# A convolution kernel: two of three images combined in place of every second, no image added by VectorE in the middle, and one more weight step after a combined low part

## The chip, the cores and the metric

The kernel runs on one core of one Trainium2 chip. The core has five engines that work side by side and meet through semaphores: TensorE (PE in the profile; PEld is its weight load), VectorE (DVE), ScalarE (ACT), GpSimd (POOL) and SyncE (SP), which only issues transfers here. Each engine runs its own instructions strictly in the order of the program. The metric is the device time of one execution in microseconds (us); lower is better. The time before is 984.07 us, the median of three runs (983.44 to 984.48).

## The reference

The input x has 160 images of 128 channels and 32 x 32 points in fp32. The output is x plus a convolution of the group-normalised x:

```
def _gn(v, G=32, eps=1e-5):
    ...
    return ((g - m) / jnp.sqrt(s + eps)).reshape(v.shape)
...
x = x + _L0_conv_ref(_gn(x), L0_conv_U)
```

The convolution is 3 x 3 with padding 1, from 128 to 128 channels, and there are five sets of weights: each run of 32 images in the kernel's order has its own. The weights are first quantised from U: `s1 = (max - min) / 3`, `v1 = s1 * floor(U / s1)`, `s2 = s1 / 5`, `v2 = s2 * floor((U - v1) / s2)`, `w = v1 + v2`.

## The kernel before, in words

**The work on one image.** The 128 channels lie on the 128 partitions, an image is 1024 elements wide, and two images are one chunk of a pool of 11 chunks. The values that TensorE multiplies are fp16, in two parts: a high part (the rounded value) and a low part (what the rounding left), each of which is multiplied with the weights. An image is handled in one of two ways, which `combined` (L607) chooses.

- A *direct* image: GpSimd normalises it into z (L670) or ScalarE does (L596, for the first images of a group), ScalarE rounds it to hi (L604), VectorE subtracts to lo (L699) and makes four quarters of sums and differences of its rows (L712, L720, L721). The high part is convolved directly: 18 matmuls at L736. The low part goes through the four quarters: 12 matmuls at L791.
- A *combined* image: the sums and differences are made before the split. GpSimd makes the edge columns (L634) and one difference (L664), VectorE the rest (L646 and L653), into a tile v of 2048 elements. ScalarE scales and rounds it to vh (L686), VectorE makes the low part vl (L692). Both parts go through the quarters: 24 matmuls at L791, and none at L736.

Of the quarters, two fill the PSUM banks m1 and m2 first (`sums_of_pairs`, L802). ScalarE copies half of m2 out (L839), and VectorE writes the sum and the difference of the two into the image's pair of banks eo (`pairs`, L848 and L850), into which `main` (L826) adds the rest. There are two such pairs of banks.

**The residual.** When an image's banks are done, one of two things happens (`by_hand`, L861, and `residual`, L868). Most images: ScalarE copies eo into a tile sum (L876), and GpSimd issues an accumulating transfer that adds sum to the image in its chunk (L899). By hand: VectorE adds eo to the image (L893). By hand are the first three, the last four, and, from image 31, every eighth. When both images of a chunk are done, SyncE stores it (L904) and loads a new one into a chunk that is free (L455).

**Statistics and weights beside the images.** ScalarE measures images ahead of their use (L202 for the mean, L209 for the square; a few by VectorE, L192). For groups of 8 images small steps on TensorE, VectorE (L257 to L270) and GpSimd (L247) make the scale. The weights of the next set are quantised on VectorE, one step at a time: `make_column` (L495) yields 14 steps for each of three columns (L101 to L127 and L507), `sums_of_set` (L544) six more (L531 to L533). The generator of these steps is called `later`, and `take(later, 1)` puts one step into VectorE's order. `later` begins at the third image of a set (the fifth in the first set), and what is left four images before the set's end is put there at once.

**The order.** One loop over the 160 images (L1039) writes all engines' instructions. The iteration of image i holds TensorE's matmuls of image i, and for VectorE in this order: the low part of image i + 2, with weight steps between, any addition by hand of image i - 1, the pair operations of image i + 1, and the sums of image i + 4 if that one is combined (or one more weight step if not). GpSimd's work for image i + 4 (`beside_pairs`, L657) is chained by `after` (L675) to the last low-part or weight step of VectorE ahead of the pair operations, so that it runs beside these; so is rstd (`power`, L245), which GpSimd does ahead of it. ScalarE's order is: measure a coming image, copy the sum of image i - 1, copy m2 of image i + 1, round the high part of image i + 3, square the coming image. SyncE's order is: store the chunk that ended at image i - 2, then load.

Of the kernel before, what the change touches and what calls it, by code (L numbers as in the profile page):

```python
# [22 lines left out]
LAST = 4  # L23
# [112 lines left out]
def last_of(steps, last=None):  # L136
    for last in steps:
        pass
    return last


def run(steps):

    while True:
        try:
            next(steps)
        except StopIteration as end:
            return end.value
# [133 lines left out]
def general_path(tc, keep, steps, x, u, out):  # L282
# [8 lines left out]
    with tc.If(far > 0), ExitStack() as ctx:  # L291
# [9 lines left out]
        for n in range(N_SETS):  # L301
            un = one.tile([P, C, TAPS], F32, tag="u", name=f"g_u{n}")
            nc.sync.dma_start(un, uv[n])
            wn = one.tile([P, C, TAPS], F32, tag="w", name=f"g_w{n}")
            k1, k2 = run(steps.quantise(one, un, f"g{n}", F32))
            nc.vector.tensor_scalar_mul(wn, k1, steps.s1)
            nc.vector.scalar_tensor_tensor(wn, k2, steps.s2, wn, ALU.mult, ALU.add)
# [38 lines left out]
class Main:  # L346
# [25 lines left out]
    LOAD_LEAD = 18  # L372
    STEADY = 7
    BY_VECTOR = (8, 10, 11, 14, 19, 24, 29, 34)
    FIFTHS = 126
    THIRDS = 146
    EARLY = 8
    FIRST = 3
    HURRIED = (0, 2, 4, 8, 24)
# [173 lines left out]
    def keep_sums(self, n, col):  # L553
        wt = self.wts[n, col]
        run(self.both_sums(
            self.nc.gpsimd, wt[:, self.SUM], wt[:, self.DIFF], *(wt[:, k] for k in range(ROW))
        ))
        if col == self.COLS[-1]:
            run(self.sums_across(n, self.nc.gpsimd))
# [47 lines left out]
    def combined(self, i):  # L607

        if i < self.STEADY or i >= self.imgs:
            return False  # L610

        if i < self.FIFTHS:
            return i % 2 == 1
        return (i - self.FIFTHS) % 5 % 2 == 0 if i < self.THIRDS else i % 3 != 1

    def by_scalar_too(self, i):

# [243 lines left out]
    def by_hand(self, i):  # L861


        if i < self.FIRST or i >= self.imgs - LAST:
            return True
        return i > self.BY_VECTOR[-1] - 4 and i % 8 == 7

    def residual(self, i):  # L868

# [38 lines left out]
    def run(self):  # L908
# [49 lines left out]
        def take(steps, count, last=None):  # L958
            for _ in range(count):
                last = next(steps, None) or last  # L960
            return last

        def measure(stage, *images):
            for i in images:
                self.measure(i, (stage,))
# [72 lines left out]
        later, turned = iter(()), []  # L1038
        for i in range(self.imgs):  # L1039
# [35 lines left out]
            if n + 1 < N_SETS:  # L1075
                if b == (2 if n == 0 else 0):
                    self.load_set(n + 1)
                if b == (4 if n == 0 else 2):
                    later = (s for col in self.COLS for s in self.make_column(n + 1, col))
# [3 lines left out]
            if i < self.FIRST:  # L1083

                if i == 0:
                    measure(0, 8, 9, 10)
                    self.normalise(4)
                    self.high_part(4)
                if i == 2:
                    self.leave(3)  # L1090
                    self.normalise(5)
                    measure(1, 9)
                    self.high_part(5)
                    self.pairs(3)
                    measure(0, 11)
                    self.low_part(4)
                    run(self.combinations(4))
                self.residual(j)
            else:

                last = None
                if self.combined(i + 2):
                    last = last_of(self.low_combined(i + 2))
                elif i + 2 < self.imgs:
                    self.low_part(i + 2)
                    take(later, 1)
                    last = last_of(self.combinations(i + 2))
                last = take(later, 1, last)
                for st in scaled:
                    self.after(st.power(), last)  # L1110
                if i + 4 < self.imgs:
                    self.beside_pairs(i + 4, last)
                if i > self.FIRST and self.by_hand(j):
                    self.residual(j)
                for k in by_scalar:
                    self.measure(k, (0,))
                if i > self.FIRST and not self.by_hand(j):
                    self.residual(j)
                    self.accumulate(j)
                part = i + 3 < self.imgs and not self.combined(i + 3)  # L1120
                if i + 1 < self.imgs:
                    self.leave(i + 1)
                for st in ready:
                    if not st.late:
                        st.deviations()
                if part:
                    if self.by_scalar_too(i + 3):
                        self.normalise(i + 3)
                    self.high_part(i + 3)
                if self.combined(i + 3):  # L1130
                    self.high_combined(i + 3)
                for k in by_scalar:
                    self.measure(k, (1,))
# [8 lines left out]
            for n_of, col in turned:  # L1142
                self.keep_taps(n_of, col)
                if col == self.COLS[-1]:
                    later = self.sums_of_set(n_of)
# [78 lines left out]
```

## Time and profile before

| what | us |
|---|---|
| median of three runs | 984.07 |
| the profiled execution's own time | 984.48 |
| its span, first to last instruction | 982.8 |
| images 35 to 138, an image on average (from the starts of L848) | 5.8 |
| start: first start of L848 (image 3) | 60.1 |

The page gives the busy time of each engine over the span, the chain of work that ended last, followed back from the last instruction, and groups of instructions: line, engine, operation, what is written and read, shapes, count, total busy time, mean of one, and the idle time of the engine just ahead of them with what ended it. The trace also gives busy times by stretch, and the waits: who waited, for what, microseconds in total, times, and the longest. A busy share is a mean over the stretch; two engines that both show nearly the whole stretch run beside each other.

### The profile page before, as it was taken

What the parts mean: (1) busy time and instruction counts of PE and PEld (TensorE: products, weight loads), DVE (VectorE), ACT (ScalarE), POOL (GpSimd) and SP (SyncE); (2) the same over time, 40 slices, a digit from 0 to 9 for tenths busy, and PEclk for the clock granted to TensorE, in tenths of its full rate; (3) what the DMA queues carried; (4) which work ended last, traced back from release to release, by engine and by line L of the source; (5) the groups of instructions that cost most, each with busy time, mean ns of one, the idle gap of its engine ahead of it and who ended that gap; (6) DMA issues with size and microseconds to landing.
All of it is one profiled execution on the core that took longest, in us unless ns stands there. A gap on an engine that the chain in (4) does not pass through costs nothing.

```text
span 982.8 us, 13226 instructions
## 1 busy us (share of the span) xinstructions
PE 944.5 (96%) x4504; PEld 442.2 (45%) x4504; DVE 913.2 (93%) x1332; ACT 830.4 (84%) x1135; POOL 355.7 (36%) x441
## 2 busy tenths in 40 slices
PE   2989999999999999999999999999999999999997
PEld 1434444444444444444444444444444444444443
DVE  7979999997999999889999998999999998989995
ACT  5759998889998998998998989898898989898551
POOL 4344423533343333333333433333333434343430
PEclk9999999999999999999999999999999999999999
DMA  9527899999998989998989999998989998997775
GB/s 354 218 84 190 219 257 256 252 267 268 279 281 268 250 262 267 265 318 229 290 222 281 240 275 270 287 258 257 258 262 246 269 265 241 316 236 202 179 205 163
DMA packets 65117, 245.86 MB, mean 250 GB/s; under 512 B 5008, under 2 KB 5008, under 8 KB 65040
## 3 DMA queue, kind: packets, MB, share of 16 engines
q1 hardware_dynamic: 45312, 173.09, 50.4%
q0 software_dynamic: 19728, 71.84, 38.1%
q8 instruction: 37, 0.61, 0.2%
q14 instruction: 40, 0.33, 0.1%
HBM read 89.19 MB, written 83.89 MB: 176 GB/s over the span
## 4 chain that ended last, share of the span: by engine, by line
PE 75%; DVE 11%; issue 4%; DMA 4%; ACT 3%; POOL 2%; SPq 0%; DVEq 0%; POOLq 0%; ACTq 0%
PE eo L736 25%; PE eo L791 24%; PE m L791 12%; PE m1b L791 8%; PE m1a L791 5%; DMA xt<-in_x_dram 2%; DVE v L646 2%; DVE vl L692 2%; DVE lo L699 1%; DVE eo L848 1%; DMA xt<-sum 1%; DMA range<-in_L_conv_U_dram 1%; POOL rstd L247 1%; DVE v L653 1%; ACT vh L686 1%
## 5 line engine op out<-in xcount | busy, mean ns | idle before, releaser
L736 PE MATMUL eo<-hi,wt 128*128 128x496 f16 (+2 forms) x1386 | 370.5, 378 | 0.9 <-ACT wt L527 0.9
L791 PEld LDWEIGHTS <-wt 128*128 128x128 f16 x1884 | 184.2, 99 | 209.9 <-DVE eo L850 1.1
L736 PEld LDWEIGHTS <-wt 128*128 128x128 f16 x1458 | 143.3, 100 | 165.9 <-issue 3.8
L202 ACT ACTIVATE junk<-xt 128x1024 f16<-128x1024 f32 x152 | 160.6, 1057 | 42.2 <-DMA xt<-in_x_dram 39.1
L692 DVE SCALAR_TENSOR_TENSOR vl<-v,rstd,vh 128x2048 f16<-128x2048 f32 x82 | 192.3, 2345 | 1.7 <-ACT vh L686 1.5
L876 ACT COPY sum<-eo 128x1024 f32<-128x1024 f32 x137 | 142.7, 1042 | 50.6 <-PE eo L791 50.4
L791 PE MATMUL eo<-vh,wt 128*128 128x496 f16 (+1 forms) x492 | 184.5, 375 | 0.3 <-DVE eo L850 0.3
L791 PE MATMUL eo<-vl,wt 128*128 128x496 f16 (+1 forms) x492 | 184.4, 375 | 0.0
L209 ACT ACTIVATE junk<-xt,mv 128x1024 f16<-128x1024 f32 x152 | 174.6, 1149 | 0.1
L791 PE MATMUL eo<-rows,wt 128*128 128x496 f16 (+1 forms) x450 | 171.6, 381 | 0.0
L686 ACT ACTIVATE vh<-v,rstd 128x2048 f16<-128x2048 f32 x82 | 164.1, 2001 | 7.3 <-DVE v L653 6.6
L791 PEld LDWEIGHTS <-across 128*128 128x128 f16 x984 | 96.2, 98 | 118.7 <-issue 7.9
L670 POOL TENSOR_SCALAR z<-xt,ngm,rstd 128x1024 f32<-128x1024 f32 x53 | 62.5, 1180 | 227.0 <-DVE rows L721 39.6
L634 POOL TENSOR_SCALAR v<-xt,ngm 128x64 f32<-128x64 f32 x82 | 30.7, 374 | 257.5 <-issue 73.6
L899 POOL DMA_DIRECT2D xt<-sum x137 | 119.6, 876 | 6.5 <-ACT sum L876 3.9
L839 ACT ACTIVATE m<-m 128x512 f32<-128x512 f32 x157 | 93.9, 598 | 22.9 <-PE m L791 16.6
L646 DVE TENSOR_TENSOR v<-xt 128x960 f32<-128x960 f32 x82 | 105.0, 1281 | 2.3 <-POOL v L634 2.3
L791 PE MATMUL m<-vl,across 128*128 128x496 f16 (+1 forms) x246 | 92.2, 375 | 4.4 <-DVE vl L692 4.3
L699 DVE TENSOR_TENSOR lo<-z,hi 128x1024 f16<-128x1024 f32 x78 | 95.0, 1217 | 0.0
L791 PE MATMUL m<-vh,across 128*128 128x496 f16 (+1 forms) x246 | 92.2, 375 | 1.1 <-ACT m L839 1.1
L664 POOL TENSOR_TENSOR v<-xt 128x512 f32<-128x512 f32 x82 | 84.7, 1032 | 0.0
L604 ACT CAST hi<-z 128x1024 f16<-128x1024 f32 x78 | 81.5, 1045 | 0.8
(144 smaller groups left out, 1156.9 us busy)
## 6 DMA issues: line engine op xcount, KB each, us to landing
xt<-in_x_dram SPq DMA_DIRECT2D x78, 1024.0 KB, 9.8
out_dram<-xt SPq DMA_DIRECT2D x78, 1024.0 KB, 5.9
xt<-sum POOLq DMA_DIRECT2D x137, 512.0 KB, 6.3
u<-in_L_conv_U_dram SPq DMA_DIRECT2D x4, 576.0 KB, 9.1
xt<-in_x_dram SPq DMA_DIRECT2D x4, 512.0 KB, 9.8
range<-in_L_conv_U_dram SPq DMA_DIRECT2D x3, 576.0 KB, 8.1
out_dram<-xt SPq DMA_DIRECT2D x3, 512.0 KB, 2.7
u<-in_L_conv_U_dram SPq DMA_DIRECT2D x2, 288.0 KB, 3.1
```

Of the source, the lines that this page charges most:

```text
L202: self.nc.scalar.activation(junk, image, ACTF.Copy, scale=-1.0 / image.shape[1], accum_out=self.mv[:, j, 0:1],)
L209: self.nc.scalar.activation(junk, image, ACTF.Square, bias=self.mv[:, j, 0:1], accum_out=self.mv[:, j, 1:2],)
L646: nc.vector.tensor_tensor(self.view(v, 1, (511, 2), (half, H), (1, half - 1)), self.view(x, 1, (1, 2), (W, H), (2, half - 1)), self.view(x ...
L664: ins = nc.gpsimd.tensor_sub(self.v[i][:, 1536:], odd, even)
L686: self.nc.scalar.mul(vh, self.v[i], st.rstd[:, j])
L692: yield self.nc.vector.scalar_tensor_tensor(vl, self.v[i], st.rstd[:, j], self.hi[i], ALU.mult, ALU.subtract)
L699: self.nc.vector.tensor_sub(lo[:, 1 : self.H + 1, :].rearrange("p h w -> p (h w)"), self.z.pop(i), self.hi[i].rearrange("p h w -> p (h w)"),)
L736: nc.tensor.matmul(self.bank(target, a)[:, first:end, c0:c1], self.wts[n, col][:, k, :], tile[:, s0 : s0 + 2 * (end - first) - 1 : 2, c0 + ...
L791: self.nc.tensor.matmul(out, weights, moving, start=start and j == 0, stop=False, skip_group_check=True)
L839: self.nc.scalar.mul(m2, self.m2_ps, 0.5)
L876: nc.scalar.copy(self.as_banks(i, self.sum[i]), self.flat(i, eo))
L899: self.nc.gpsimd.dma_start(self.image(i), self.sum.pop(i), accum_op=ALU.add)
```

## The change

The choice of combined images becomes one rule for all images from the eighth on: i % 3 is not 1. Before it was every odd image to 125, then three of five to 145, then the same rule as now. `by_hand` loses its middle: images 31, 39, 47 and so on to 151 go through ScalarE's copy and the accumulating transfer like the others. After the low part of a combined image two weight steps are taken in place of one; after a direct one it stays at two (one between the low part and its quarters, one behind them). GpSimd's instructions of `beside_pairs` and `power` stay chained to the last of these.

```diff
     def combined(self, i):
...
-        if i < self.FIFTHS:
-            return i % 2 == 1
-        return (i - self.FIFTHS) % 5 % 2 == 0 if i < self.THIRDS else i % 3 != 1
+        return i % 3 != 1
...
     def by_hand(self, i):
-        if i < self.FIRST or i >= self.imgs - LAST:
-            return True
-        return i > self.BY_VECTOR[-1] - 4 and i % 8 == 7
+        return i < self.FIRST or i >= self.imgs - LAST
...
-                last = take(later, 1, last)
+                last = take(later, 2 if self.combined(i + 2) else 1, last)
                 for st in scaled:
                     self.after(st.power(), last)
                 if i + 4 < self.imgs:
                     self.beside_pairs(i + 4, last)
```

The constants `FIFTHS = 126` and `THIRDS = 146` go, since nothing reads them.

More of the change, by code (lines that the diff above doesn't have):

```diff
@@ L374 @@
     BY_VECTOR = (8, 10, 11, 14, 19, 24, 29, 34)
-    FIFTHS = 126
-    THIRDS = 146
     EARLY = 8
```

## The prediction

> **What bounds the kernel now.** I read the page from the top: the busy shares first, then the chain that ended last, then the busy times by stretch, because the shares are means over stages with different limits.
>
> ```profile
> span 982.8 us, 13226 instructions
> PE 944.5 (96%) x4504; PEld 442.2 (45%) x4504; DVE 913.2 (93%) x1332; ACT 830.4 (84%) x1135; POOL 355.7 (36%) x441
> PE 75%; DVE 11%; issue 4%; DMA 4%; ACT 3%; POOL 2%; SPq 0%; DVEq 0%; POOLq 0%; ACTq 0%
> ```
>
> TensorE holds three quarters of the chain, but VectorE is only 3 points less busy. The stretches below (stretch, then PE, PEld, DVE, ACT and POOL busy with counts, clock, DMA share, GB/s) say where each one decides.
>
> ```profile
> 67.00:163.00 96.00, 92.92 (x449) 43.56 (x448) 94.24 (x155) 85.38 (x118) 36.81 (x44) 1.00 0.86 236
> 163.00:258.00 95.00, 93.35 (x448) 43.69 (x447) 87.02 (x127) 84.79 (x119) 36.86 (x46) 1.00 0.99 268
> 443.00:581.00 138.00, 138.00 (x664) 64.64 (x663) 135.81 (x201) 124.66 (x174) 49.27 (x57) 1.00 0.94 260
> 581.00:628.00 47.00, 47.00 (x227) 22.13 (x226) 40.44 (x57) 43.14 (x59) 16.48 (x19) 1.00 0.98 278
> ```
>
> The last two rows are one set of 32 images (185 us, 5.78 us an image). For about 24 images the next set's weights are quantised on VectorE between the images: TensorE is full, and VectorE is idle for only 2.2 us of 138. For the other 8, VectorE has 6.6 us free in 47. So the middle is bound by TensorE with VectorE 2% behind it, and in 67 to 163 VectorE is already the fuller one. The change takes from the first and gives to the second, so its whole worth hangs on that 2%.
>
> **The change part by part.** The groups that it touches (line, engine, operation, shapes, count; busy us and mean ns; idle before):
>
> ```profile
> L692 DVE SCALAR_TENSOR_TENSOR vl<-v,rstd,vh 128x2048 f16<-128x2048 f32 x82 | 192.3, 2345 | 1.7 <-ACT vh L686 1.5
> L646 DVE TENSOR_TENSOR v<-xt 128x960 f32<-128x960 f32 x82 | 105.0, 1281 | 2.3 <-POOL v L634 2.3
> L699 DVE TENSOR_TENSOR lo<-z,hi 128x1024 f16<-128x1024 f32 x78 | 95.0, 1217 | 0.0
> L653 DVE SCALAR_TENSOR_TENSOR v<-xt,twice 128x512 f32<-128x512 f32 x82 | 60.8, 742 | 0.0
> ...
> L712 DVE TENSOR_TENSOR rows<-lo 128x1024 f16<-128x1024 f16 x75 | 51.3, 684 | 0.8
> L721 DVE TENSOR_TENSOR rows<-lo 128x512 f16<-128x512 f16 x75 | 31.2, 416 | 0.0
> L720 DVE TENSOR_TENSOR rows<-lo 128x512 f16<-128x512 f16 x75 | 31.2, 416 | 0.0
> L893 DVE TENSOR_TENSOR xt<-eo,xt 128x1024 f32<-128x1024 f32 x21 | 25.6, 1217 | 4.3 <-PE eo L791 3.3 <-PE eo L736 1.0
> ```
>
> Back-to-back records overlap by about 0.08 us: in the timeline L692 starts at 354.64 and its successor at 356.90. So I price by the distance from one start to the next: L692 2.26, L646 1.23, L653 0.66, together 4.15 us for a combined image; L699 1.13, L712 0.60, L720 and L721 0.33 each, together 2.40 for a direct one.
>
> *More combined images.* By the old rule 60 images to 125, 12 in 126 to 145 and 10 after are combined: 82, as L692 counts. By the new one, every i from 7 with i % 3 not 1: 102. For each of the 20: TensorE runs 24 matmuls instead of 30. In the chain of waits twelve of them take 2.54 us, so a combined image is 5.08; a direct one is six steps of 0.85 (three L736 and one L791) and six L791 of 0.65 per three, 6.40. That is 1.32 us saved. VectorE pays 4.15 less 2.40, 1.75 us more. ScalarE pays L686 (2.00) for L604 (1.05), 0.95 more. GpSimd pays L634 and L664 (0.37 and 1.03) for L670 (1.18), 0.2 more; at 36% busy that hides. Totals: PE -26, DVE +35, ACT +19.
>
> *None added by VectorE in the middle.* Images 31, 39 and so on to 151, sixteen, lose L893. Its record is 1.22, start to start about 1.35 with its wait on PE: DVE -21 us. In its place come sixteen ScalarE copies (1.04 each, L876: ACT +16), sixteen GpSimd issues (L899, 0.88 each: POOL +14, hidden), and 16 transfers of 512 KB. The 137 of before take 38.1% of 16 engines' 983 us, 2.73 us each, so DMA +44 us. In the present middle the engines are 0.94 to 0.98 busy, so this has little cover.
>
> *One more weight step after a combined low part.* A set has 48 steps (three columns of 14, six sums). Two per image are taken now, alternating 1 and 3; afterwards 7 in three images, so they end after 20.6 images, not 24. Their sum, about 22.5 us a set (0.47 each, from the spacing of L101 to L127, L507 and L531 to L533), is moved, not added. But GpSimd's rstd, edge columns and difference are chained to the last of these steps, and start one step (0.47 us) later. L646 waits for the edge columns; the two pair operations between (1.33 us) cover their 0.37, but not rstd and edges together (1.47 and 0.37). Today that wait is 2.3 us in 4 places. I take +1 us in all; without the pair operations' cover it would be 0.5 us for each of 102 images.
>
> *Buffers* move no wait that I can see: the two v buffers now serve neighbours, but each is read for the last time an iteration before it is written again.
>
> *Sum for one set of the middle* (185.0 us now). VectorE's content apart from the steps in the first 24 images is 135.8 less 22.5, over 24: 4.72 us an image. Add 1.75/6 (half to two thirds combined) and take off 1.35/8: 4.84. Over 20.6 images, with the steps, 122.2 us; the idle share that VectorE has where it is already the fuller (1.8 of 96 us, first row) makes it 124.4. The other 11.4 images: TensorE falls by 1.32/6 to 5.56; ScalarE is at 43.1/8 = 5.39 now and gains 0.16 and 0.13, 5.68 as record time, less as spacing. I take 5.62, 64.1 us. Sum 188.5, so +3.5 for each of three sets, **+10.5**. With no idle share and 5.56 it would be +0.6 a set; with 5% idle and 5.75, +9.
>
> *First set (60 to 259 us).* 18 combined in place of 14: VectorE +7, less 1.35 for image 31, about 4 of it where VectorE is the fuller; the steps brought forward cost it there and are given back after. TensorE's -5 counts only in the second half, which waits elsewhere. **+4** (0 to +8).
>
> *From 813 us on.* One more combined, three adds less, no weight steps: TensorE -1.3 and some of VectorE's -4 where it holds the chain. **-2.5** (-5 to +1).
>
> The total is +12. The profiled execution took 984.48 us, its span 982.8 and 1.7 around it, and 0.4 above the median of 984.07. 984.5 + 12 = **996.5**, so I say **997**. A measurement tells 0.2%, 2 us, from no change.
>
> **Two rules against rows.** The matmuls start every 0.21 us with no gap in 443 to 628, so I count TensorE's saving in full where it decides. The Trainium skill (Perfetto Trace Analysis, Identifying the Most-Contended Engine) warns that matmul busy time is no measure of headroom and wants the weight-load share instead. That is 45% here, and read so, TensorE would not be the limit, the 11.4 images would stay at today's 47/8 = 5.88, 0.26 above my 5.62, and three sets would add 9 us, an estimate of 1006. I follow the starts.
>
> L646's record runs from 1149 to 1989 ns, longer where GpSimd's L664 lies beside it; my 1.23 is a spacing with GpSimd beside it. The Trainium skill (SBUF — State Buffer, Who interferes with whom) says that a VectorE instruction with two SBUF inputs contends with GpSimd's reads; by it the new L646 could cost the upper end, 0.7 us more for 20, +14 us. No row makes that usual.
>
> **The rivals.**
> 1. *VectorE runs ahead* (faster). If its surplus is absorbed by running ahead while TensorE has less to do, a set costs its total only: 176.3 + 5.33 x 1.75 - 4 x 1.35 = 180.2, with today's 2.2 idle 182.4, -2.6 a set; with the first set at 0 and the end at -4 that is 973. For it: VectorE at 98% and TensorE at 100% live beside each other now. Against: its order is fixed, pair operations wait for one of two PSUM pairs, and the 6.6 us free are where no weights are due, images away. It decides when more than 4 us a set are carried over.
> 2. *The accumulating transfers bind* (much slower). SyncE's stores wait for them in order, and the loads stand behind the stores:
>
> ```profile
> SPq L904 <- DMA xt<-sum: 760.4, 84, 16.0
> SPq L455 <- DMA out_dram<-xt: 25.8, 14, 2.6
> ```
>
> and ScalarE's first pass over an image waits for the load (who waited for what: us in total, times, longest):
>
> ```profile
> ACT junk L202 <- DMA xt<-in_x_dram: 39.1, 24, 8.1
> ```
>
> Every fourth chunk now has its last image added by VectorE and catches up there. From 163 to about 240 us every image is accumulated already, and the stretch 163 to 258 shows DMA 0.99, 9.3 us of ScalarE's waits for loads (its waits in that window), TensorE 1.65 us idle and VectorE 8. Four transfers more make a set's DMA 0.95 x 185 + 10.9 = 187 us, above the time it has. If ScalarE's late copies hold VectorE's pair operations for 1.65 to 3 us in 95, that is +10 to +18 over some 570 us of the middle, on top of the forecast's 997 in part, since VectorE waits already there: 1010. Against: the shares reach 1.03 with 310 GB/s elsewhere.
> 3. *The terms cancel*: +0.6 a set, +1 in the first, -3 at the end: 984.
>
> **How the numbers follow.** Forecast 0.50, rival 2 0.22, rival 1 0.17, rival 3 0.11. The forecast's own terms give 986 to 1010; the range reaches down into rival 1 and up to rival 2's figure: 979 to 1012. Faster is 0.17 from rival 1 and 0.02 of rival 3, same 0.08 of rival 3, the rest slower, 0.73.
>
> **What would show it.** L692 x102, L893 x5, L876 x153; matmuls 120 fewer. Right: in a set's first 21 images VectorE without gaps at about 6.0 us an image and TensorE with gaps, then 5.6 an image. Wrong towards faster: TensorE still without gaps with weights in the stretch. Wrong towards slower: L202's waits for loads well above 39 us, or L848 waiting for ScalarE above its 31 us of before.

## The result, and the profile after

The changed kernel takes 1043.7 us (median of four), before takes 983.8: the ratio is 1.061, with a 95% interval of 1.059 to 1.064. The loss is 60 us, and the prediction, which had the direction, put it at 12; the time lies above its range. The lines move by four to six in the new file: L692 is now L688, L646 is L642, L653 is L649, L848 and L850 are L844 and L846, L876 is L870, L899 is L893 and L904 is L898.

The top of the page of after, in the order in which that of before was read:

```profile
span 1041.6 us, 13067 instructions
PE 938.9 (90%) x4384; PEld 427.6 (41%) x4384; DVE 940.6 (90%) x1296; ACT 853.0 (82%) x1139; POOL 382.6 (37%) x489
DVE 45%; DMA 18%; issue 15%; PE 10%; POOL 7%; ACT 4%; SPq 0%; POOLq 0%; ACTq 0%; DVEq 0%
```

TensorE has 120 matmuls fewer (4384 for 4504), as it should, but the chain went from TensorE (75% to 10%) to VectorE (45%) and to transfers (18%). No engine is busier than 90%, so the span is made of stretches with different limits. Here are the stretches of the same images as in the prediction (images 4 to 18 and 19 to 34 of the first set, then 67 to 90 and 91 to 98); columns as there: stretch, length, PE, PEld, DVE, ACT and POOL busy, clock, DMA share, GB/s.

```profile
66.00:174.00 108.00, 96.92 (x448) 43.75 (x446) 103.35 (x162) 87.21 (x117) 37.01 (x49) 0.97 0.80 216
174.00:273.00 99.00, 93.42 (x441) 43.30 (x440) 85.81 (x112) 86.02 (x119) 40.46 (x51) 0.98 0.94 247
472.00:622.00 150.00, 136.25 (x637) 61.34 (x635) 143.29 (x196) 128.25 (x174) 56.15 (x67) 0.99 0.95 254
622.00:672.00 50.00, 47.81 (x219) 21.88 (x219) 40.97 (x52) 45.11 (x60) 17.61 (x21) 0.97 0.99 268
```

Images 67 to 90, most of them beside weight steps, took 138 us and now take 150. TensorE, which had no gap there, has 14 us of them, and VectorE is busy for 143. Images 91 to 98, without weight steps, took 47 and now take 50, though TensorE has less to do there, VectorE is idle for 9, and the DMA engines are at 0.99. These are two different losses, and the experiments were made to part them.

Where the 58.8 us of span came from, by the starts of the pair operations: the part to image 34 took 14.7 us more (1.2 less up to image 3, 15.9 more from there), images 35 to 130, three sets' worth, 41.9 more (554.9 to 596.8), and the rest 2.2 more. The prediction had 4, 10.5 and -2.5.

The groups of VectorE that grew, and the waits that answer to those shown of before:

```profile
L688 DVE SCALAR_TENSOR_TENSOR vl<-v,rstd,vh 128x2048 f16<-128x2048 f32 x102 | 239.2, 2345 | 3.0 <-ACT vh L682 2.7
L642 DVE TENSOR_TENSOR v<-xt 128x960 f32<-128x960 f32 x102 | 136.2, 1336 | 7.2 <-POOL v L630 7.2
L649 DVE SCALAR_TENSOR_TENSOR v<-xt,twice 128x512 f32<-128x512 f32 x102 | 75.7, 742 | 4.3 <-POOL twice L279 4.3
```

```profile
ACT junk L202 <- DMA xt<-in_x_dram: 59.1, 34, 7.8
...
DVE eo L844 <- ACT m L835: 36.9, 25, 3.6
PE m L787 <- DVE vl L688: 36.4, 24, 5.4
...
DVE nnn L101 <- DMA u<-in_L_conv_U_dram: 6.6, 3, 4.0
```

TensorE's wait for the low part was in before:

```profile
PE m L791 <- DVE vl L692: 4.3, 4, 1.3
```

The counts are as forecast (102). One duration is not: the difference that was 1281 ns is 1336. TensorE now waits for VectorE's low part 36 us in 24 places (4.3 in 4 before), and ScalarE's waits for loads went from 39 to 59 us. The load of the next set's U stands in the same queue of SyncE: VectorE's first weight step waits for it three times, which it did not in before.

### The profile page after: what moved, and what is told of

Its sections match the earlier page's. It is cut to its first block, busy times and chain, and to the rows that moved or that the text cites. A ratio compares the mean times of both kernels' runs of the same rounds, so it can differ in the third digit from the quotient of the medians.

```text
span 1041.6 us, 13067 instructions
## 1 busy us (share of the span) xinstructions
PE 938.9 (90%) x4384; PEld 427.6 (41%) x4384; DVE 940.6 (90%) x1296; ACT 853.0 (82%) x1139; POOL 382.6 (37%) x489
## 4 chain that ended last, share of the span: by engine, by line
DVE 45%; DMA 18%; issue 15%; PE 10%; POOL 7%; ACT 4%; SPq 0%; POOLq 0%; ACTq 0%; DVEq 0%
DVE vl L688 11%; DVE v L642 7%; DMA xt<-in_x_dram 7%; DMA xt<-sum 7%; DVE eo L844 5%; DMA u<-in_L_conv_U_dram 4%; PE eo L787 4%; DVE v L649 4%; DVE lo L695 3%; DVE eo L846 3%; PE eo L732 2%; POOL rstd L247 2%; PE m L787 2%; DVE tt L110 1%; POOL v L660 1%
## 5 line engine op out<-in xcount | busy, mean ns | idle before, releaser
L787 PEld LDWEIGHTS <-wt 128*128 128x128 f16 x1884 | 181.8, 99 | 231.8 <-DVE eo L846 15.9
L732 PE MATMUL eo<-hi,wt 128*128 128x496 f16 (+3 forms) x1026 | 273.5, 377 | 2.6 <-DVE eo L846 1.6
L688 DVE SCALAR_TENSOR_TENSOR vl<-v,rstd,vh 128x2048 f16<-128x2048 f32 x102 | 239.2, 2345 | 3.0 <-ACT vh L682 2.7
L787 PE MATMUL eo<-vh,wt 128*128 128x496 f16 (+1 forms) x612 | 230.7, 377 | 4.1 <-DVE eo L846 3.8
L787 PE MATMUL eo<-vl,wt 128*128 128x496 f16 (+1 forms) x612 | 230.6, 377 | 0.0
L682 ACT ACTIVATE vh<-v,rstd 128x2048 f16<-128x2048 f32 x102 | 203.9, 1999 | 31.1 <-DVE v L649 20.8
L202 ACT ACTIVATE junk<-xt 128x1024 f16<-128x1024 f32 x152 | 160.6, 1057 | 62.2 <-DMA xt<-in_x_dram 59.1
L870 ACT COPY sum<-eo 128x1024 f32<-128x1024 f32 x153 | 160.8, 1051 | 40.2 <-PE eo L787 39.8
L732 PEld LDWEIGHTS <-wt 128*128 128x128 f16 x1098 | 106.7, 100 | 127.4 <-DVE eo L846 8.5
L787 PE MATMUL m<-vl,across 128*128 128x496 f16 (+1 forms) x306 | 117.6, 384 | 36.5 <-DVE vl L688 36.4
L642 DVE TENSOR_TENSOR v<-xt 128x960 f32<-128x960 f32 x102 | 136.2, 1336 | 7.2 <-POOL v L630 7.2
L893 POOL DMA_DIRECT2D xt<-sum x153 | 133.6, 873 | 10.6 <-ACT sum L870 9.6
L787 PE MATMUL eo<-rows,wt 128*128 128x512 f16 x330 | 126.0, 382 | 0.0
L660 POOL TENSOR_TENSOR v<-xt 128x512 f32<-128x512 f32 x102 | 105.1, 1030 | 0.0
L844 DVE SCALAR_TENSOR_TENSOR eo<-m1b,m 128x512 f32<-128x512 f32 x79 | 54.9, 695 | 34.9 <-ACT m L835 26.6
L649 DVE SCALAR_TENSOR_TENSOR v<-xt,twice 128x512 f32<-128x512 f32 x102 | 75.7, 742 | 4.3 <-POOL twice L279 4.3
```

Of the source, the lines that this page charges most:

```text
L202: self.nc.scalar.activation(junk, image, ACTF.Copy, scale=-1.0 / image.shape[1], accum_out=self.mv[:, j, 0:1],)
L642: nc.vector.tensor_tensor(self.view(v, 1, (511, 2), (half, H), (1, half - 1)), self.view(x, 1, (1, 2), (W, H), (2, half - 1)), self.view(x ...
L649: nc.vector.scalar_tensor_tensor(v[:, 1024:1536], even, st.twice[:, j], odd, ALU.add, ALU.add)
L660: ins = nc.gpsimd.tensor_sub(self.v[i][:, 1536:], odd, even)
L682: self.nc.scalar.mul(vh, self.v[i], st.rstd[:, j])
L688: yield self.nc.vector.scalar_tensor_tensor(vl, self.v[i], st.rstd[:, j], self.hi[i], ALU.mult, ALU.subtract)
```

## The experiments

Two theories were put against each other. **V**: VectorE is full beside weight steps, so what it is given there lengthens the time in full, and what TensorE saves is lost. **T**: an image's accumulating transfer gates its chunk's store on SyncE, the store gates the load queued behind it, and a late load holds ScalarE, which then copies late. A third, **D**, comes up later: the DMA engines as a whole cannot move more. Ratios are to before on the same chip, with 95% intervals.

**One part at a time.**

*The adds alone:*

```diff
-        if i < self.FIRST or i >= self.imgs - LAST:
-            return True
-        return i > self.BY_VECTOR[-1] - 4 and i % 8 == 7
+        return i < self.FIRST or i >= self.imgs - LAST
```

> Before, with one part of the change alone: images 31, 39 to 151 are no longer added by VectorE. Theory T (transfers): each accumulating transfer gates its chunk's store on SyncE, the store gates the load behind it, and a late load holds ScalarE; every eighth image by VectorE let this chain catch up. It expects 8 to 25 us slower (992 to 1009), with L202's waits for loads up from 39 us. Theory V (VectorE's content): VectorE loses 16 times 1.35 us, the time is the same or up to 6 us shorter (978 to 984).

993.6 us, ratio 1.010 (1.007 to 1.013), 9.7 us more. VectorE is busy 18 us less than in before, and the kernel is slower: that is T's number, and V alone does not hold. The run leaves two rivals, which a later one settles: ScalarE has 16 copies more, and the DMA engines 16 transfers more. ScalarE's waits in that run:

```profile
ACT junk L202 <- DMA xt<-in_x_dram: 68.4, 44, 8.4
```

They were 39.1 in 24 places.

*The second step alone:*

```diff
-                last = take(later, 1, last)
+                last = take(later, 2 if self.combined(i + 2) else 1, last)
```

> Before, with a second weight step after each combined low part and nothing else: 5 steps in two images in place of 4, the rule of the images and the adds stay. Theory V expects VectorE to be the fuller in the weight stretches, 19 images at about 6.0 us a set instead of 24 at 5.84, and the rest at 5.8: 0 to 8 us slower (984 to 992). Theory T expects nothing beyond 2 us.

996.3 us, ratio 1.013 (1.010 to 1.015), 12.4 us more, above V's 8, although not one instruction is added. Images 67 to 90 and 91 to 98 of that run:

```profile
450.00:591.00 141.00, 139.34 (x665) 64.16 (x664) 137.25 (x202) 123.79 (x174) 49.58 (x58) 1.00 0.92 254
591.00:638.00 47.00, 47.00 (x227) 22.14 (x226) 40.31 (x55) 43.87 (x60) 16.42 (x20) 1.00 0.99 282
```

The same work of VectorE is drawn together in fewer images: the first 16 of these run at 6.16 us each with VectorE idle for 0.1 (5.87 before), and the images set free run no faster than TensorE lets them. A set lost 3 us, and the part to image 34 as much. ScalarE's waits for loads are longer here too (53.6 us for 39.1), so a part of the 12.4 may be the chain's; no run parts that. Work moved out of an image pays only if the image it leaves had VectorE as its limit; here that limit was TensorE.

*The rule with the step, the adds put back* (after with the old `by_hand`). The rule without the second step was not tried: it takes five steps in three images, so a set's 48 would need some 29 images, and what is left four images before the set's end is put there at once. What follows is therefore the rule on top of the step.

> After, with the adds by VectorE of images 31, 39 to 151 put back: the rule i % 3 and the second step stay. Theory V expects it slower than after, since VectorE gets 16 adds of 1.35 us back, 1044 to 1064. Theory T expects most of the middle's loss gone: 16 us stay in the first set, which has no such adds, and the middle is 10 to 20 us above before: 1005 to 1022.

1032.7 us, ratio 1.049 (1.047 to 1.052): 36.4 us more than with the step alone. Both theories missed: it is faster than after, against V, but nowhere near T's 1005 to 1022. The same images:

```profile
469.00:620.00 151.00, 137.21 (x642) 61.96 (x641) 145.88 (x198) 126.91 (x172) 53.67 (x64) 0.99 0.90 245
620.00:666.00 46.00, 43.96 (x208) 20.37 (x208) 41.93 (x53) 42.69 (x58) 16.76 (x21) 1.00 0.94 267
```

VectorE is busy 146 of 151 us beside the steps, and the DMA engines only 0.90; in the eight images without steps the time is 46, a little better than before's 47. So the rule's loss is all beside the steps, and it is VectorE's. Taken in this order the parts are 12.4 (step), 36.4 (rule) and 11.0 us (adds, from this run to after). The order matters little to the adds: taken first they cost 9.7.

**The loads' place in SyncE's order.**

```diff
-            self.store(i - 2)
             while loaded * NB < min(self.imgs, i + self.LOAD_LEAD):
                 self.load(loaded)
                 loaded += 1
+            self.store(i - 2)
```

In after:

> After, with SyncE's loads put ahead of the store in each iteration, so that a load no longer stands behind a store that waits for an accumulating transfer. Theory T: L202's waits for loads fall from 59 us to below 25, the stretches without weight steps go from about 6.1 us an image to 5.7, 15 to 30 us faster than after (1014 to 1029). Theory V: VectorE's content is the limit, at most 5 us faster (1039 to 1044).

1027.7 us (1019 to 1029 in four), ratio 1.042 (1.037 to 1.047), 16 us faster than after, as T expected; the weight stretches stay (images 67 to 82: 6.36 us each, 6.37 in after), and images 59 to 66 go from 6.05 to 5.78.

In before:

> Before, with SyncE's loads ahead of the store in each iteration. Theory T says the same chain costs before a little: ScalarE's 39 us of waits for loads fall below 25, and the stalls of TensorE near 200 to 225 and 800 us shrink: 2 to 8 us faster (976 to 982). Theory V expects no change (982 to 986).

989.5 us, ratio 1.006 (1.003 to 1.009): slower, a miss for both. A load may now stand ahead of a store and wait there for the store that frees its chunk, and what is behind it on SyncE waits too, the next set's U among it. VectorE's first weight step waited for that (waits in 400 to 470 us):

```profile
DVE nnn L101 <- DMA u<-in_L_conv_U_dram: 7.2, 1, 7.2
```

**Without weight steps.** Sets 1 to 4 take the weights of set 0 (`load_set` and `make_column` are not called; the tables are handed on). The same 150 us of the middle are shown for all.

> Before, without the weight steps: sets 1 to 4 use set 0's weights, so their quantisation on VectorE (some 22 us a set), the reload of U, the turning on TensorE and the copies on ScalarE are left out. TensorE bounds before in the middle in either theory, so it gains little there: TensorE's own 36 turning matmuls and the stretch near 100 to 160 us, where VectorE is the fuller: 960 to 976.

975.0 us, ratio 0.991 (0.989 to 0.992). VectorE is busy 81 us less (832.6), and the time is only 9.6 shorter, since TensorE bounds.

```profile
472.00:622.00 150.00, 150.00 (x718) 70.20 (x716) 127.77 (x173) 135.75 (x185) 53.95 (x62) 1.00 0.93 264
```

> After, without the weight steps in the same way. VectorE's content falls to about 5.05 us an image, below TensorE's 5.56. If VectorE's content alone made after slower (theory V), this is faster than before without steps by most of TensorE's 26 us: 935 to 955. If the transfers' chain holds an image at 5.9 to 6.1 without steps too (theory T), it is slower than before without steps: 975 to 1000.

1002.0 us, ratio 1.018 (1.016 to 1.021), slower as T expected and 2 us above its range. VectorE and TensorE both have room, the DMA engines do not:

```profile
472.00:622.00 150.00, 143.06 (x665) 65.44 (x664) 126.78 (x154) 131.66 (x175) 57.40 (x69) 0.98 0.98 262
```

So the change costs 60 us with the weight steps and still 27 without them (975.0 to 1002.0). VectorE is idle for 23 of the 150 us here, so the 27 are not for want of its time; the 33 that go with the steps are the part that needs a full VectorE.

> After, without the weight steps (left out as in the run before) and with the loads ahead of the store. Theory T: the chain is cut, 5.6 to 5.75 us an image, 20 to 40 us faster than after without steps alone (940 to 965). Theory V: VectorE is not the limit here and the order of SyncE matters little, within 8 us of after without steps.

1010.8 us, ratio 1.027 (1.022 to 1.032): no faster, so T as I had put it failed here. SyncE's waits show why (the trace is of the fastest of the four, 1004.9):

```profile
SPq L453 <- DMA out_dram<-xt: 658.1, 69, 14.0
SPq L898 <- DMA xt<-sum: 163.8, 30, 11.2
```

In after without steps they were

```profile
SPq L898 <- DMA xt<-sum: 821.9, 94, 14.8
```

The wait has only changed its name (658.1 and 163.8 make the same 822): the loads now wait for the store that frees their chunk, and that store had waited for its accumulating transfer. In after with steps the order helped, perhaps because the weight stretches leave the transfers time to get ahead; that is not tested.

The adds put back, every eighth image and then every fourth (i % 4 == 3):

> After without weight steps (left out as in the runs before: sets 1 to 4 use set 0's weights), with the adds by VectorE of images 31, 39 to 151 put back. Theory D (DMA throughput): with every image accumulated, the records of the 16 engines need about 5.85 us an image, which is what after without steps takes; with seven of eight they need 5.5, and TensorE's 5.56 decides: 5.6 to 5.7 us an image, 954 to 968, faster than before without steps (975). Theory V or ScalarE as the limit: VectorE gets 16 adds, no faster than 1002.

969.2 us, ratio 0.984 (0.983 to 0.986): 33 us faster than without the adds, 1 us above D's range, and below before without steps.

> The same with every fourth image from 31 added by VectorE in place of every eighth. Theory D: the DMA engines need 5.2 us an image, VectorE 5.4, TensorE stays the limit: within 6 us of the run with every eighth. If the transfers still decided with every eighth, this is faster by 8 us or more.

962.3 us, ratio 0.978 (0.977 to 0.980). It is 7 us faster still, so the transfers were not quite out of the way with every eighth.

```profile
472.00:622.00 150.00, 149.48 (x716) 70.07 (x715) 142.42 (x177) 138.63 (x184) 56.10 (x68) 1.00 0.92 255
```

TensorE is full again, at 5.5 to 5.7 us an image. Here TensorE's saving from the rule can be seen for once: 975.0 to 962.3. From image 35 to 130 it is 17 us (553.8 to 536.7), where the forecast's 0.22 us an image would be 21; the first set gives 6 of it back. The adds alone cannot have done it, since before without steps had no gap on TensorE there.

**Which image is added, not how many.** In before:

```diff
-        return i > self.BY_VECTOR[-1] - 4 and i % 8 == 7
+        return i > self.BY_VECTOR[-1] - 4 and i % 8 == 6
```

> Before, with the images 38, 46 and so on (i % 8 == 6) added by VectorE in place of those with i % 8 == 7. The number of transfers is the same but for one; the last image of its chunk is now accumulated in every chunk. Theory T (the chain from the chunk's last accumulating transfer through the store to the load): no chunk catches up any more, about as slow as with no adds at all, 990 to 996. Theory D (throughput): no change, 981 to 987.

992.5 us, ratio 1.009 (1.007 to 1.011), as slow as with no adds at all. There is one transfer more than in before, and VectorE still makes 15 of the 16 adds; but they are the first images of their chunks, and the chunk's store waits for the second. Neither the throughput of the DMA engines nor ScalarE's work (one copy more) explains that; the chain does:

```profile
ACT junk L202 <- DMA xt<-in_x_dram: 78.8, 44, 8.0
```

The adds also move into other iterations of VectorE, those of a combined low part, and that could be a rival. It is not the cause: where VectorE is full the run is no slower than before (images 67 to 82 take 5.82 us each for 5.87), and where it loses, VectorE is idle for more than in before (0.40 us an image for 0.09 in images 83 to 90, 1.05 for 0.82 in 91 to 98).

**The rule only where there are no steps.**

```diff
-            return i % 2 == 1
+            b = self.place(i)[1]
+            return i % 3 != 1 if i >= 32 and (b < 3 or b > 26) else i % 2 == 1
```

> Before, with the rule i % 3 only for images from 32 whose iterations hold no weight steps (place in the set under 3 or over 26; 126 and after follow as they do before), the adds and the steps as before. VectorE has 0.8 us an image free there and the DMA engines need 5.5. If VectorE's content in the weight stretches and the DMA engines are what made after slower, TensorE's 0.22 us an image comes through here: 974 to 982. If the rule itself (two combined images in a row) costs, it is slower than before: 986 to 995.

983.6 us, ratio 1.000 (0.999 to 1.001). Neither number: the rule itself costs nothing there, and TensorE's gain does not come. Only four more images are combined here (86 for 82), so 4 times 1.32, some 5 us, were at stake. ScalarE's waits for loads were 60 us, so I took the chain for what ate this gain; the last run below does not bear that out in full.

**The issue's place in GpSimd's order.** From the end of ScalarE's copy to GpSimd's issue of the transfer there are 3.0 us in before and 3.7 in after (medians, from the records of `sum` and of `xt<-sum`), because GpSimd first does rstd, edge columns and difference, which wait for VectorE's last step. The block that copies and issues was put ahead of them:

```diff
-                for st in scaled:
-                    self.after(st.power(), last)
-                if i + 4 < self.imgs:
-                    self.beside_pairs(i + 4, last)
                 ...
                     self.residual(j)
                     self.accumulate(j)
+                for st in scaled:
+                    self.after(st.power(), last)
+                if i + 4 < self.imgs:
+                    self.beside_pairs(i + 4, last)
```

> Before, with GpSimd's issue of the accumulating transfer of image i - 1 (and ScalarE's copy ahead of it) put ahead of rstd and of the edge columns, difference or z of image i + 4 in GpSimd's order. If the 3.0 us (median) between the copy's end and the issue are part of the chain, ScalarE's waits for loads fall below 25 us: 2 to 8 us faster (975 to 981). If the transfers themselves are what is late, or if GpSimd's work now waits for the copy and holds VectorE's L646, no faster (982 to 992).

981.9 us, ratio 0.998 (0.997 to 1.000): 1.4 us, less than the least that I expected. The issue now follows the copy by 0.3 us, and the waits all but went:

```profile
ACT junk L202 <- DMA xt<-in_x_dram: 10.5, 4, 7.8
```

In before these waits cost little: TensorE is the limit there, with no gap from 443 to 628 us, and ScalarE had room for them.

> After, with the same change of GpSimd's order. Chain: its share of the loss is 10 to 16 us (adds alone +10, loads first -16), and the issue comes 3.7 us earlier of some 20: 6 to 14 us faster than after (1029 to 1037), most of it in the stretches without weight steps (6.0 to 6.2 us an image now). The weight stretches (6.36) do not move, since VectorE is full there. If GpSimd's delay is no part of it: 1040 to 1050.

1030.8 us, ratio 1.049 (1.048 to 1.051): 13 us faster than after, as the chain expected. Images 67 to 82 stay at 6.4 us, 83 to 90 go from 6.0 to 5.7 and 91 to 98 from 6.2 to 5.95. The waits of that run:

```profile
ACT junk L202 <- DMA xt<-in_x_dram: 20.2, 10, 7.4
...
DVE v L642 <- POOL v L630: 11.4, 14, 1.4
```

The second line is the price: VectorE waits for the edge columns 11.4 us, where it was 7.2.

**A version that beats both.** Thirds where there are no steps, and there also every fourth image added by VectorE:

```diff
-        return i > self.BY_VECTOR[-1] - 4 and i % 8 == 7
+        b = self.place(i)[1]
+        free = i >= 128 or b < 3 or b > 26
+        return i > self.BY_VECTOR[-1] - 4 and (i % 8 == 7 or free and i % 4 == 3)
```

> Before, with i % 3 where the iterations hold no weight steps (as in the run before this one) and there also every fourth image added by VectorE (i % 4 == 3, so the last of every second chunk). VectorE then has 5.4 us an image there, TensorE 5.56. If the chain is what ate the gain of thirds there (ScalarE's waits for loads were 60 us), they fall below 45 and this is 3 to 9 us faster than before (975 to 981); if not, 982 to 988.

980.8 us, ratio 0.998 (0.997 to 0.999), at the weak end of what was expected; the waits for loads fell only from 60 to 54.5 us.

> The last one with the accumulating issue ahead of GpSimd's other work as well. If both help apart, 970 to 978; if the earlier issue only moves the wait to VectorE's L646, 981 to 992.

979.2 us, ratio 0.996 (0.994 to 0.998): 4 us faster than before, less than the sum that I had named, and the fastest version that computes the whole reference. The waits for loads are down to 10.1 us here, as in the run with the issue moved in before (10.5), and it is 2.7 us faster than that run. So even without those waits only about half of the 5 us of the thirds comes through; where the rest goes is open.

## Why the prediction was wrong

**The direction was right, and half of the place.** "The change takes from the first and gives to the second, so its whole worth hangs on that 2%" is what happened beside the steps: VectorE took the chain, and TensorE's 26 us are not to be seen in the time. The counts came as forecast. The totals of busy time less so: VectorE was to gain 14 us (35 less 21) and gained 27, ScalarE 35 and gained 23. Both signs that were named for wrong towards slower came: L202's waits for loads (59 us for 39) and the waits of L848, now L844, for ScalarE (37 for 31).

**The step that failed is the sum for one set**: 188.5 us was forecast, 199.8 measured (images 67 to 98), 11.3 short. It failed in two terms.

*Beside the steps.* The forecast was 20.6 images at 6.04 and the next 3.4 at 5.62, 143.5 us for images 67 to 90; they took 150. I had VectorE's content at 5.93 us an image; in images 67 to 82 it was busy 6.19, with 0.18 idle, so 6.37 for my 6.04. Of these 0.33 us, the weight steps are 0.10 (38 steps of 0.50 us in 16 images, where I had 37 of 0.47), L642 is 0.09 (1.37 us from its start to the next, where I had 1.23), and the idle time 0.07 (2.8%, where I took 1.8% from the first set). The remaining 0.07 I have not parted. The run with the step alone showed at 12 us what the "moved, not added" steps cost. The runs with and without steps give the size: with the adds kept the change costs 49 us with steps (983.9 to 1032.7) and gains 6 without (975.0 to 969.2).

Behind the longer L642 stands a term that I had put at +1 us in all: GpSimd's work starts one step later. L642 waited for the edge columns 7.2 us in 10 places (2.3 in 4 before), in the iterations where GpSimd does rstd first. Each of these ten times, and once more, its own record was some 1.98 us long, because GpSimd's difference L660 had begun just ahead of it; before had 4 such records. Together that is some 10 us more of VectorE's time in the whole run. The step alone does not do it (2.3 us in 4 places in that run, and 4 long records).

*Without the steps.* 5.62 us an image was forecast, from TensorE and ScalarE; 6.2 came (images 91 to 98). Here I had the right rival and gave it 0.22: "The accumulating transfers bind". Its mechanism was seen ("Every fourth chunk now has its last image added by VectorE and catches up there"), and the run with even images shows just that. Its price, 10 to 18 us, was of the right size too: putting the adds back saves 11.0, the earlier issue 13, the loads first 16. What the even images speak against is the reason by throughput beside it (187 us a set); it is a chain: copy, issue, landing, store, load, landing, ScalarE's pass. And I put it beside the forecast as another case, on top of it only in part, while both losses hold at once, in different stretches; their sum (997 and the 10 to 18 of that rival) would have been 1007 to 1015 still, so most of the miss is VectorE's. In images 91 to 98 a third thing has a small share: for 3.4 us from 622.4 us TensorE ran at half its clock, which costs it some 1.7 us of the 50.

*The first set* lost 15.9 from image 3 on, for 4. VectorE is busy 8.6 us more in images 3 to 26, and idle there for 6 us more. Part of that idle time is a wait for GpSimd that was not there before, since images 8 and 24 are combined now and are the first of their groups (L649 for `twice`, 1.9 and 2.5 us); the rest I have not parted.

*The end* lost 2.2 for a gain of 2.5: images 131 to 138 ran at 5.9 for 5.7, with VectorE idle 0.7 an image; no run parts that.

**The two rules.** The Trainium skill's page Perfetto Trace Analysis (Identifying the Most-Contended Engine) warns against matmul busy time; it names MFU (the matmul work done, as a share of the peak) beside the weight-load share, and I had used the second alone. The 1006 that I read from it was nearer than 997 by luck: with the chain and VectorE out of the way, TensorE's saving came through (962.3 for 975.0), so TensorE was a limit. The rule of SBUF — State Buffer (Who interferes with whom), that a VectorE instruction with two SBUF inputs contends with GpSimd's reads, agrees with L642: in after its records took 1152 ns where GpSimd's L660 did not overlap them (28) and 1405 where it did (74). The mean went from 1281 to 1336 ns; over 102 that is 5.6 us and not the 14 that I had as its end.

**What stays open.** How much of the chain is the transfers' own landing and how much is queueing on SyncE, no run parts. The landing took 6.3 us (median) in before, 6.9 in after and 7.8 in after without steps. It took 7.1 in before with the issue moved ahead, so a transfer that is issued 2.7 us earlier does not land 2.7 us earlier. Nor do the runs part the chain from the DMA engines' throughput in after without steps, where these are at 0.98.

## What to carry to other kernels

When two engines both fill a stretch, work taken from one and given to the other can be a loss of nearly the whole gift (here 36 us for 41 us more of VectorE's busy time), and moving the fuller engine's work earlier can be a loss too (12 us here); sum each stretch by its own engine and by how the work really falls on its iterations, not by the mean. Look in the queue of the engine that issues stores and loads for what each of them waits for: an operation that looks like spare work (here every eighth add by the busiest engine) may be the one that keeps a chain of transfers from holding the whole loop. And two losses in different stretches add up; they are not rivals.

## What the runs showed of the hardware

The granted clock of TensorE was 0.987 over the span of after and 0.994 over that of before. It fell in pieces of 3.4 us at half: in after there are seven between 62 and 797 us, each beside a gap of TensorE of 2.05 to 5.41 us, and in before one in that stretch, at 64 us, beside a gap of 4.3. Not every such gap has one (that of 3.2 us ahead of 344 us in after has none). In such a piece the matmuls start 0.42 us apart in place of 0.21:

```profile
622.00:626.00 4.00, 3.62 (x10) 1.32 (x10) 3.57 (x8) 3.97 (x5) 0.89 (x1) 0.57 1.02 307
```

The landing time of the same 512 KB did not go by the mean load on the DMA engines alone: it was 6.3 us in before and 7.2 in the run with even images, with the engines busy for 0.89 of both spans.

VectorE's difference of two SBUF inputs (L642) was held up by GpSimd's L660, and not the other way round: L660 began first in all 74 overlaps and kept its 1.03 us, while L642 took its 1.15 us and about the length of the overlap less 0.13 us on top (0.16 for an overlap of 0.29, 0.83 for 0.97).
